# A selective scan with a third kind of state, one block for the activation functions of other tables, and Softplus and Silu taken from PSUM

## The chip, the cores and the metric

The kernel runs on one core of one Trainium2 chip. The metric is the device time of one execution in microseconds (us), taken over several runs. A core has a matrix engine (TensorE, PE in the profile), a vector engine (VectorE, DVE), an engine for activation functions (ScalarE, ACT), a general engine (GpSimd, POOL), and a queue that only issues transfers (SyncE, SP). Each engine works through its own instructions in the order in which the program put them there, and waits at an instruction until what it needs has been signalled by other engines. SBUF is the working memory, PSUM the small memory that TensorE writes into; it has eight banks of 128 x 512 f32.

## The reference

There are two layers with residuals. Layer 0 is a two-dimensional recurrent cell over a 64 x 64 image for 16 batches; the change does not touch it. Layer 1 is a bidirectional selective scan (Mamba) over the 4096 tokens of each batch, with 256 inner channels and 16 states per channel:

```python
xz = x @ in_w.T
xc, z = jnp.split(xz, 2, axis=-1)
# xc: causal convolution with 4 taps, + conv_b
xc = jax.nn.silu(...)
dbl = xc @ x_w.T
dt, Bm, Cm = jnp.split(dbl, [8, 24], axis=-1)
dt = jax.nn.softplus(dt @ dt_w.T + dt_b)
A = -jnp.exp(A_log)
dA = jnp.exp(dt[..., None] * A)
dBx = dt[..., None] * Bm[:, :, None, :] * xc[..., None]
# over the tokens:
h = dA_t * h + dBx_t
y = jnp.einsum('bds,bs->bd', h, C_t)
# then
y = (ys + xc * D) * jax.nn.silu(z)
return y @ out_w.T
```

The same is done on the reversed tokens, and both results are added. All is f32.

## The kernel before

Layer 1 cuts the tokens of a batch into 8 chunks of 512. One *pass* is one chunk in one direction: 16 batches x 2 directions x 8 chunks make 256 passes, the first 8 of a batch forward, the other 8 ("second") backward. A pass keeps the channels as 2 halves of 128 partitions, and treats the 16 states one after another. For state s it needs the decay exp(dt A) (two ScalarE instructions of 128 x 512, `decay`, line 482), the drive dt B x, two scans along the tokens on VectorE (`scan`, line 515), the product with C (`out_of`, line 539), and a sum over the states that TensorE makes by transposing each product into one PSUM accumulator `py` (`sums`, line 561, 8 transposes of 128 x 128).

Before, there are two kinds of state. Ten are *plain*: GpSimd multiplies dt x by the row of B (`drive`, line 492), the decay lies in PSUM (tag `da`, three banks), the scan writes `hst` into SBUF (two buffers), GpSimd multiplies by C, and ScalarE copies the last column into `carry` for the next chunk (`keep`, line 533). Six are *turned* (2, 4, 7, 9, 12, 15): ScalarE multiplies the transposed dt x by B as a scalar per partition (`drive_turned`, line 497, four instructions), TensorE turns the result back into two PSUM banks `hps` (`drive_back`, line 505, 8 transposes; there is one such tile), VectorE scans in place there with a decay in SBUF (`das`, two buffers), multiplies by C and copies the last column.

Around the states a pass does its own preparation one pass ahead: the convolution as 4 shifted matmuls for each half (`conv`), Silu on it in SBUF, `xproj` for dt, B and C, a round trip of B and C through DRAM, from where each row is spread over 128 partitions by a transfer on SP (`spread`, line 435), `dtproj`, Softplus in SBUF after an Identity that added the bias (lines 453 to 459), and dt x (`times`, on GpSimd). Second passes also make the gate z (copied from PSUM, then Silu in SBUF), add both directions and multiply by z (`finish`, two VectorE instructions; the forward passes copy `py` to `yf` on ScalarE instead), and project back.

Nothing is scheduled by a compiler: every step has a place, counted in states, in the tables `AT` and `STATE` (lines 639 to 682). All steps of all passes are put into one list, sorted by place, and issued in that order; so a table entry decides where an instruction stands in its engine's queue. The eight PSUM banks are `misc` 1, `da` 3, `hps` 2 and `py` 2.

Of the kernel before, what the change touches and what calls it, by code (L numbers as in the profile page):

```python
# [231 lines left out]
def layer1(tc, a, const, ident, group_norm, x1, out):  # L232
# [8 lines left out]
    with ExitStack() as ctx:  # L241
# [62 lines left out]

        TURNED = (2, 4, 7, 9, 12, 15)
        B_ROWS, C_ROWS = 6, 5
        PLAIN = tuple(s for s in range(NS) if s not in TURNED)

        def misc(name):
            return psum.tile([P, T], F32, name=name, tag="misc")
# [37 lines left out]
        class Pass:  # L350
            def __init__(self, b, n):
                self.b, self.n = b, n
                self.d, self.c = order[n]
                self.second = n >= NCH
                self.first = n % NCH == 0
                self.nm = f"{b}_{n}"
                self.rev = slice(None, None, -1 if self.d else 1)
                self.last = 0 if self.d else T - 1
                self.brow, self.crow, self.da, self.dbx, self.dbt = {}, {}, {}, {}, {}
                self.h, self.hlast, self.hc, self.das = {}, {}, {}, {}  # L360
                self.banks = set()
                self.added = 0
                self.py = None

# [13 lines left out]
            def conv_take(self, h):  # L378
                if h == 0:
                    self.xc = cp.tile([P, NH, T], F32, name=f"xc_{self.nm}", tag="xc")  # L380
                nc.scalar.activation(self.xc[:, h, :], self.pp, AF.Identity, bias=conv_b[:, h, :])  # L381

            def gate(self, i):

                pp = self.pp = psum.tile([P, 2, DI], F32, name=f"pz_{self.nm}_{i}", tag="misc")
                for j in range(2):
                    t0 = PAD + self.c * T + (2 * i + j) * P
                    nc.tensor.matmul(  # L388
                        pp[:, j, :],
                        lhsT=xT[self.b % 2][:, t0 : t0 + P],  # L390
                        rhs=in_wT[:, DI:],
                        start=True,
                        stop=True,
                    )

            def gate_take(self, i):
                if i == 0:
                    self.z = cp.tile([P, NB, DI], F32, name=f"z_{self.nm}", tag="z")
                nc.scalar.copy(self.z[:, 2 * i : 2 * i + 2, :], self.pp)

            def silu(self):
                nc.scalar.activation(self.xc, self.xc, AF.Silu)
                if self.second:
                    nc.scalar.activation(self.z, self.z, AF.Silu)

            def xproj(self):
                pd = self.pp = psum.tile([NDBL, T], F32, name=f"pd_{self.nm}", tag="misc")
# [33 lines left out]
                nc.sync.dma_start(t, src)  # L441

            def dtproj(self, h):
                pv = self.pp = misc(f"pv_{self.nm}_{h}")
                nc.tensor.matmul(  # L445
                    pv,
                    lhsT=dt_wT[:, h * P : (h + 1) * P],
                    rhs=self.dbl[:RANK, :],
                    start=True,
                    stop=True,  # L450
                )

            def dtproj_take(self, h):
                if h == 0:
                    self.dt = cp.tile([P, NH, T], F32, name=f"dt_{self.nm}", tag="dt")
                nc.scalar.activation(self.dt[:, h, :], self.pp, AF.Identity, bias=dt_b[:, h, :])  # L456

            def softplus(self):
                nc.scalar.activation(self.dt, self.dt, AF.Softplus)

            def times(self):
                self.dtx = cp.tile([P, NH, T], F32, name=f"dtx_{self.nm}", tag="dtx")
# [17 lines left out]


            def decay(self, s, h):
                if s in TURNED:
                    if h == 0:
                        self.das[s] = sp.tile([P, NH, T], F32, name=f"das_{self.nm}_{s}", tag="das")
                    t = self.das[s][:, h, :]
                else:
                    t = psum.tile([P, T], F32, name=f"da_{self.nm}_{s}_{h}", tag="da", bufs=3)
                nc.scalar.activation(t, self.dt[:, h, :], AF.Exp, scale=amat[:, h, s : s + 1])  # L489
                self.da[s, h] = t  # L490
# [24 lines left out]
            def scan(self, s):  # L515
                dbx = self.dbx.pop(s)
                if s in TURNED:
                    t = dbx
                else:
                    t = sp.tile([P, NH, T], F32, name=f"hst_{self.nm}_{s}", tag="hst", bufs=2)  # L520
                for h in range(NH):
                    nc.vector.tensor_tensor_scan(  # L522
                        t[:, h, self.rev],
                        self.da.pop((s, h))[:, self.rev],
                        dbx[:, h, self.rev],
                        0.0 if self.first else carry[:, self.d, h, s : s + 1],
                        ALU.mult,
                        ALU.add,
                    )
                self.h[s] = t  # L530
                self.hlast[s] = t

            def keep(self, s):
                (nc.vector.tensor_copy if s in TURNED else nc.scalar.copy)(
                    carry[:, self.d, :, s : s + 1],
                    self.hlast.pop(s)[:, :, self.last : self.last + 1],
                )
# [97 lines left out]
        def put(place, f, *args):  # L635
# [1 line left out]


        AT = {
            "conv": (-15.8, -14.5),  # L640
            "conv_take": (-14.7, -13.4),
            "gate": (-13.3, -12.8),
            "gate_take": (-12.9, -12.5),
            "silu": -12.27,
            "xproj": -10.87,
            "xproj_take": -10.08,
            "bturn": -9.79,
            "bturn_take": -9.49,
            "dtproj": (-9.25, -8.75),
            "dtproj_take": (-8.98, -8.48),  # L650
            "softplus": -8.17,
            "times": -6.08,
            "turn": (-5.39, -4.79),
            "turn_take": (-5.25, -4.34),
            "skip": (4.22, 4.93, 7.62, 8.2),
            "finish": 18.96,
            "residual": 15.49,
            "back": (19.6, 20.45),
            "back_take": (20.1, 20.7),
            "project": 24.0,  # L660
            "project_take": 24.49,
            "store": 25.98,
            "store_take": 26.48,
            "read_load": 3.57,
            "read_turn": 12.07,
            "read_take": 12.57,
            "normal": -2.75,
            "normalise": -1.31,
        }

        STATE = {
            "decay_turned": (-1.78, -1.23),
            "decay_plain": (-1.52, -0.92),
            "drive_turned": -2.2,
            "drive_back": -1.07,
            "out_turned": 0.16,
            "out_plain": 1.06,
            "keep_turned": 0.1,
            "keep_plain": 1.55,
            "sums_turned": 2.13,  # L680
            "sums_plain": 3.22,
        }

        plain = [(i, p, s) for i, p in enumerate(passes) for s in PLAIN]
# [2 lines left out]
        def many(i, p, name, n, f):  # L687
            for k in range(n):
                put(NS * i + AT[name][k], f, k)

        for i, p in enumerate(passes):
            at = NS * i
            many(i, p, "conv", NH, p.conv)
            many(i, p, "conv_take", NH, p.conv_take)
            if p.second:
                many(i, p, "gate", NB // 2, p.gate)
                many(i, p, "gate_take", NB // 2, p.gate_take)
            many(i, p, "dtproj", NH, p.dtproj)
            many(i, p, "dtproj_take", NH, p.dtproj_take)
            many(i, p, "turn", NB // 2, p.turn)  # L700
            many(i, p, "turn_take", NB // 2, p.turn_take)
            many(i, p, "skip", NB, p.skip)
            for name in ("silu", "xproj", "xproj_take", "bturn", "bturn_take", "softplus", "times"):
                put(at + AT[name], getattr(p, name))
            put(at + AT["finish"], p.finish)
            if p.second:
                many(i, p, "back", NH, p.back)
                many(i, p, "back_take", NH, p.back_take)
# [12 lines left out]
                        put(at + AT["normal"], normal, p.b + 1)  # L721
                    put(at + AT["normalise"], normalise, p.b + 1, p.n - NCH)
            for s in range(NS):
                kind = "turned" if s in TURNED else "plain"
                for h in range(NH):
                    put(at + s + STATE["decay_" + kind][h], p.decay, s, h)
                put(at + s, p.scan, s)
                put(at + s + STATE["keep_" + kind], p.keep, s)
                put(at + s + STATE["out_" + kind], p.out_of, s)
                put(at + s + STATE["sums_" + kind], p.sums, s)  # L730
                if s in TURNED:
                    put(at + s + STATE["drive_turned"], p.drive_turned, s)
                    put(at + s + STATE["drive_back"], p.drive_back, s)

        drive_at = []
        for k, (i, p, s) in enumerate(plain):
            if k < 2:
                at = NS * i + s - 2.5  # L740
            else:
                i2, _, s2 = plain[k - 2]
                at = NS * i2 + s2 + STATE["out_plain"] + 0.01
            drive_at.append(at)
            put(at, p.drive, s)
            ready = NS * i + AT["xproj_take"] + 0.01
# [1 line left out]
            put(max(ready, free), p.spread, "b", s)  # L748
        out_at = []
        for k, (i, p, s) in enumerate(every):  # L750
            out_at.append(NS * i + s + STATE["out_turned" if s in TURNED else "out_plain"])
            ready = NS * i + AT["xproj_take"] + 0.02
            free = out_at[k - C_ROWS] + 0.01 if k >= C_ROWS else ready
            put(max(ready, free), p.spread, "c", s)
# [40 lines left out]
```

## Time and profile before

| what | us |
|---|---|
| median of 3 runs | 15579.79 |
| lowest, highest | 15575.36, 15591.93 |
| the profiled execution | 15566.78 |
| its span on the core | 15565.0 |
| the first scan of layer 1 starts | 1623.3 |
| the last scan of layer 1 starts | 15544.0 |

The 256 passes lie between the two last entries: 13920.7 us, or 54.4 us for a pass. Busy shares of the engines over the span are PE 82%, DVE 87%, ACT 79%, POOL 82%; in a stretch of 1000 us of layer 1 alone (5000 to 6000) they are 80%, 89%, 83% and 89%. The granted clock of TensorE is 0.899 on average over the span. The DMA engines are busy 42% of that stretch. A profile of this kind lists for each group of instructions its line, engine, operation, output and input, count, then the busy time and the mean duration, then the idle time of the engine before it and what ended that idle time.

### The profile page before, as it was taken

The numbers are of one execution on the slowest core, as the hardware profiler recorded it, in microseconds if no ns is written. First come the engines' busy times: TensorE is split into PE (matmuls) and PEld (weight loads), VectorE is DVE, ScalarE is ACT, GpSimd is POOL, SyncE is SP. The second block draws the span as 40 slices with busy tenths as digits, with TensorE's granted clock in tenths as the row PEclk, the third lists the DMA queues.
The fourth block names the chain that finished last, engine by engine and source line by source line (L and its number), as shares of the span: only waits on it lengthen the run. The fifth ranks groups of instructions, "written<-read, shape, count | busy, mean of one in ns | idle before, by whom it ended". The sixth has DMA issues, their size and how long they took to land. (4 is left out here: it accounts for less than half of the span.)

```text
span 15565.0 us, 215358 instructions
## 1 busy us (share of the span) xinstructions
PE 12706.6 (82%) x68876; PEld 9322.4 (60%) x68876; DVE 13558.3 (87%) x14526; ACT 12256.2 (79%) x23207; POOL 12705.8 (82%) x5636
## 2 busy tenths in 40 slices
PE   8999778788878778887878888887878878787887
PEld 8658555556555555555555655555565655555555
DVE  6777789889898989899898989888898989898898
ACT  3444788888888888888888888888888888888887
POOL 0111889889898989899898989889898989899898
PEclk8999888888898988898889989888988988888998
DMA  3211444444444444444444444444444444444443
GB/s 115 55 54 43 130 129 138 132 136 135 131 139 128 142 128 139 131 137 136 131 139 128 142 128 139 132 134 134 135 136 131 142 129 139 129 138 133 133 135 121
DMA packets 1335631, 1978.89 MB, mean 127 GB/s; under 512 B 136664, under 2 KB 465888, under 8 KB 1334496
## 3 DMA queue, kind: packets, MB, share of 16 engines
q1 hardware_dynamic: 1256560, 1929.88, 39.1%
q10 hardware_dynamic: 77936, 35.23, 0.9%
q8 instruction: 546, 8.95, 0.2%
q14 instruction: 589, 4.83, 0.1%
HBM read 1880.69 MB, written 83.89 MB: 126 GB/s over the span
## 5 line engine op out<-in xcount | busy, mean ns | idle before, releaser
L543 POOL TENSOR_TENSOR hc<-hst,cr 128x1024 f32<-128x1024 f32 x2560 | 6047.6, 2362 | 1424.1 <-DVE hst L522 562.4
L494 POOL TENSOR_TENSOR dbx<-dtx,br 128x1024 f32<-128x1024 f32 x2560 | 6054.1, 2365 | 0.1
L522 DVE TENSOR_TENSOR_SCAN hst<-da,carry,dbx 128x512 f32<-128x512 f32 x4480 | 5475.8, 1266 | 462.1 <-ACT da L489 238.2
L551 PE MATMUL py<-ident,hc 128*128 128x128 f32 x32768 | 4409.1, 288 | 45.9 <-DVE y L582 40.5
L551 PEld LDWEIGHTS py<-ident,hc 128*128 128x128 f32 x32768 | 4039.9, 151 | 224.6 <-issue 187.7
L489 ACT ACTIVATE da<-dt,A_log_sb 128x512 f32<-128x512 f32 x5120 | 3443.4, 684 | 848.9 <-DVE hst L522 834.1
L522 DVE TENSOR_TENSOR_SCAN hps<-das,carry,hps 128x512 f32<-128x512 f32 x2688 | 3441.3, 1280 | 564.3 <-issue 224.6
L510 PE MATMUL hps<-ident,dbt 128*128 128x128 f32 x12288 | 2223.4, 323 | 884.0 <-DVE hc L543 452.0
L510 PEld LDWEIGHTS hps<-ident,dbt 128*128 128x128 f32 x12288 | 1701.9, 164 | 1582.5 <-ACT dbt L500 714.2
L500 ACT ACTIVATE dbt<-dtxt,bt 128x256 f32<-128x256 f32 x6144 | 2618.3, 499 | 0.0
L489 ACT ACTIVATE das<-dt,A_log_sb 128x512 f32<-128x512 f32 x3072 | 2113.0, 711 | 0.2
L370 PE MATMUL pp<-xT,wk 128*128 128x512 f32 x4096 | 1873.3, 600 | 190.6 <-ACT xc L381 188.3
L543 DVE TENSOR_TENSOR hc<-hps,cr 128x1024 f32<-128x1024 f32 x1536 | 1881.0, 1225 | 144.6 <-PE py L551 111.0
L370 PEld LDWEIGHTS pp<-xT,wk 128*128 128x128 f32 x4096 | 739.2, 190 | 985.7 <-issue 740.7
L196 POOL TENSOR_TENSOR a_f<-a_f,c 128x8 f32<-128x8 f32 (+31 forms) x254 | 199.3, 785 | 1348.4 <-ACT a_f L188 1172.1
L551 PEld LDWEIGHTS py<-ddiag,xc 128*128 128x128 f32 x4096 | 676.2, 231 | 366.0 <-issue 366.0
L470 PE MATMUL ptx<-ident,dtx 128*128 128x128 f32 x2048 | 372.2, 311 | 634.2 <-POOL dtx L463 382.8
L445 PE MATMUL pv<-dbl,dt_wT 8*128 8x512 f32 x1024 | 695.3, 764 | 199.5 <-ACT dt L456 199.2
L522 DVE TENSOR_TENSOR_SCAN hst<-da,dbx 128x512 f32<-128x512 f32 x640 | 742.5, 1206 | 112.6 <-ACT da L489 78.4
L551 PE MATMUL py<-ddiag,xc 128*128 128x128 f32 x4096 | 794.1, 326 | 0.0
L479 ACT COPY dtxt<-ptx 128x512 f32<-128x512 f32 x512 | 299.1, 584 | 551.2 <-PE ptx L470 550.8
L470 PEld LDWEIGHTS ptx<-ident,dtx 128*128 128x128 f32 x2048 | 270.6, 161 | 700.6 <-POOL dtx L463 417.9
(110 smaller groups left out, 13755.2 us busy)
## 6 DMA issues: line engine op xcount, KB each, us to landing
cr<-rows SPq DMA_DIRECT2D x4096, 256.0 KB
br<-rows SPq DMA_DIRECT2D x2560, 256.0 KB
xs<-in_x_dram SPq DMA_DIRECT2D x64, 512.0 KB
xl<-x SPq DMA_DIRECT2D x128, 256.0 KB
xr<-x SPq DMA_DIRECT2D x128, 256.0 KB
out_dram<-xr SPq DMA_DIRECT2D x128, 256.0 KB
xl<-in_x_dram SPq DMA_DIRECT2D x392, 64.0 KB
x<-xl ACTq DMA_DIRECT2D x392, 64.0 KB
```

What stands on the lines that cost most here:

```text
L196: nc.gpsimd.tensor_mul(f0, f0, cp[:, up, :])
L370: nc.tensor.matmul(pp, lhsT=wk[:, k, h * P : (h + 1) * P], rhs=xT[self.b % 2][:, t0 : t0 + T], start=(k == 0), stop=(k == TAPS - 1),)
L445: nc.tensor.matmul(pv, lhsT=dt_wT[:, h * P : (h + 1) * P], rhs=self.dbl[:RANK, :], start=True, stop=True,)
L470: nc.tensor.transpose(pt[:, j, h * P : (h + 1) * P], self.dtx[:, h, (2 * i + j) * P : (2 * i + j + 1) * P], ident,)
L479: nc.scalar.copy(self.dtxt[:, 2 * i : 2 * i + 2, :], self.pp)
L489: nc.scalar.activation(t, self.dt[:, h, :], AF.Exp, scale=amat[:, h, s : s + 1])
L494: nc.gpsimd.tensor_mul(t, self.dtx, bc(self.brow.pop(s), 1, NH))
L500: nc.scalar.activation(t[:, j, :], self.dtxt[:, j, :], AF.Copy, scale=self.bt[:, j, s : s + 1])
L510: nc.tensor.transpose(t[:, h, j * P : (j + 1) * P], dbt[:, j, h * P : (h + 1) * P], ident)
L522: nc.vector.tensor_tensor_scan(t[:, h, self.rev], self.da.pop((s, h))[:, self.rev], dbx[:, h, self.rev], 0.0 if self.first else carry[:, s ...
L543: eng.tensor_mul(t, self.h.pop(s), bc(self.crow.pop(s), 1, NH))
L551: nc.tensor.matmul(self.py[:, j, h * P : (h + 1) * P], start=j // 2 not in self.banks, stop=self.added >= (NS + 1 - 1) * NB * NH, skip_gro ...
```

## The change

Four states become a third kind, *mixed*: B on ScalarE and TensorE as for turned states, the scan from PSUM into SBUF, C on GpSimd as for plain states. Four are turned, four mixed, eight plain. `keep` of plain and mixed states is no longer a ScalarE copy but a transfer on SP. Silu of xc, Softplus and Silu of z stand in one block (`session`) in each pass, for three different passes; Softplus and Silu of z read PSUM directly, and their inputs take `misc` and one of the three `da` banks. `hst` has three buffers. All places are new; `finish` follows the last `sums`, and nothing that writes `py` for the next pass is put before it.

```diff
-        TURNED = (2, 4, 7, 9, 12, 15)
+        TURNED = (2, 8, 10, 14,)
+        MIXED = (0, 5, 7, 11,)
+        PLAIN = tuple(s for s in range(NS) if s not in TURNED and s not in MIXED)
...
             def gate_take(self, i):
...
-                nc.scalar.copy(self.z[:, 2 * i : 2 * i + 2, :], self.pp)
-            def silu(self):
-                nc.scalar.activation(self.xc, self.xc, AF.Silu)
-                if self.second:
-                    nc.scalar.activation(self.z, self.z, AF.Silu)
+                nc.scalar.activation(self.z[:, 2 * i : 2 * i + 2, :], self.pz[i], AF.Silu)
...
-            def dtproj_take(self, h):
-                nc.scalar.activation(self.dt[:, h, :], self.pp, AF.Identity, bias=dt_b[:, h, :])
             def softplus(self):
-                nc.scalar.activation(self.dt, self.dt, AF.Softplus)
+                for h in range(NH):
+                    nc.scalar.activation(
+                        self.dt[:, h, :], self.pv[h], AF.Softplus, bias=dt_b[:, h, :]
+                    )
...
             def decay(self, s, h):
-                if s in TURNED:
+                if s not in PLAIN:
...
-                    t = sp.tile([P, NH, T], F32, name=f"hst_{self.nm}_{s}", tag="hst", bufs=2)
+                    t = sp.tile([P, NH, T], F32, name=f"hst_{self.nm}_{s}", tag="hst", bufs=3)
...
             def keep(self, s):
-                (nc.vector.tensor_copy if s in TURNED else nc.scalar.copy)(
+                (nc.vector.tensor_copy if s in TURNED else nc.sync.dma_start)(
...
+        def session(i):
+            at = [passes[k] if 0 <= k < len(passes) else None for k in (i, i + 1, i + 2)]
+            if at[0] and at[0].second:
+                at[0].gate_take(0)
+            if at[1]:
+                at[1].dtproj(0)
+            if at[0] and at[0].second:
+                at[0].gate_take(1)
+            if at[2]:
+                at[2].silu()
+            if at[1]:
+                at[1].softplus()
...
-            many(i, p, "skip", NB, p.skip)
+            for j in range(NB):
+                put(max(at + AT["skip"][j], finished), p.skip, j)
...
+                summed = max(at + s + STATE["sums_" + k], finished)
+                lasts = max(lasts, summed)
+                put(summed, p.sums, s)
...
+            finished = lasts + 0.01
+            put(finished, p.finish)
```

The new tables, as far as the prediction speaks of them (places in states, from the pass's own first scan):

```diff
-            "conv": (-15.8, -14.5),
+            "conv": (-27.32, -26.22),
-            "finish": 18.96,
+            "session": 9.8,
...
-            "drive_back": -1.07,
-            "sums_turned": 2.13,
-            "sums_plain": 3.22,
+            "drive_mixed": -2.2,
+            "drive_back": -0.55,
+            "sums_turned": 1.95,
+            "sums_mixed": 3.94,
+            "sums_plain": 3.72,
```

## The prediction

> **What bounds the kernel now.** I read the page's busy shares first, then the busy time by windows, then the groups by line, then the timeline of two passes. The shares show no single bound.
>
> ```profile
> 5000.00:6000.00 1000.00, 801.47 (x4456) 588.61 (x4454) 894.35 (x855) 830.89 (x1553) 893.49 (x385) 0.90 0.42 135
> ```
>
> ```profile
> L543 POOL TENSOR_TENSOR hc<-hst,cr 128x1024 f32<-128x1024 f32 x2560 | 6047.6, 2362 | 1424.1 <-DVE hst L522 562.4
> L494 POOL TENSOR_TENSOR dbx<-dtx,br 128x1024 f32<-128x1024 f32 x2560 | 6054.1, 2365 | 0.1
> ```
>
> The window's columns are the busy us of PE, PEld, DVE, ACT and POOL, then clock, DMA share and GB/s. Of a pass of 54.4 us, DVE is busy 48.6 (89.4%), POOL 48.6, ACT 45.2, PE 43.6. POOL and DVE are equal, and each idles nearly 6 us, because they feed each other through two or three buffers and both hang on ACT. The timeline shows where a stall starts:
>
> ```profile
> 9019.05 1.28 ACT L402 ACT_TABLE_LOAD   x1
> ...
> 9020.35 1.06 ACT L402 ACTIVATE xc<-xc 128x1024 f32<-128x1024 f32 x1
> ...
> 9021.31 1.04 ACT L404 ACTIVATE z<-z 128x1024 f32<-128x1024 f32 x1
> ...
> 9022.37 1.28 ACT L489 ACT_TABLE_LOAD   x1
> 9023.66 1.30 ACT L489 ACTIVATE da<-dt,A_log_sb 128x512 f32<-128x512 f32 x2
> 9024.39 2.34 DVE L522 TENSOR_TENSOR_SCAN hst<-da,dbx 128x512 f32<-128x512 f32 x2 [1.98 <-ACT da L489]
> ...
> 9025.74 2.36 POOL L543 TENSOR_TENSOR hc<-hst,cr 128x1024 f32<-128x1024 f32 x1 [2.36 <-issue]
> ```
>
> For 4.6 us ACT makes no exponential; the scan then waits 1.98 us for its decay, and POOL 2.36 us for the scan. The same happens again at Softplus, so twice in a pass. The two halves of a batch differ, which the starts of the yf copies show:
>
> ```profile
> L578 ACT COPY yf<-py x8: 999/1001/1002, 8651.7 to 9015.7; 128x1024 f32<-128x1024 f32 x8
> ...
> L578 ACT COPY yf<-py x6: 999/1000/1002, 9522.3 to 9777.6; 128x1024 f32<-128x1024 f32 x6
> ```
>
> Seven intervals in the first line give 52.0 us for a forward pass. From 9015.7 to 9522.3 lie nine passes, mostly second ones: 56.3 us.
>
> **What the Trainium skill says.** "ScalarE: Activation LUTs", section "What ACT_TABLE_LOAD costs", has 1283 ns for a load, plus a drain of about 1380. The trace agrees on the load (1283) but shows no such drain: from load to next function is 1.30 us above. "GPSIMD Engine Reference", section "Performance versus the Vector engine", makes a two-input product 1.96 times as slow as on VectorE; here 2362 to 1225 ns, 1.93. "DMA: Bandwidth & Descriptors", section "Anatomy of one DMA", says a transfer has about 2.0 us of fixed cost and that the issuing sequencer, not the DMA engine, waits for semaphores. No transfer of 4-byte elements is in this trace; the rows of B and C take SP 0.32 us each to issue.
>
> **The change part by part**, in us per pass.
>
> *GpSimd.* 10 B + 10 C + dt x before, 8 B + 12 C + dt x after: 21 products either way. Back to back they start every 2.32 us (9028.06, 9030.39, 9032.70), so 48.7 is its floor before and after. Nothing is saved here.
>
> *VectorE.* Two turned states less: two products with C of 1.225 and two copies of 0.16, -2.8: 48.6 becomes 45.8. A mixed scan (decay SBUF, drive PSUM, result SBUF) isn't in the trace; its neighbours are 1.266 and 1.280, and I take 1.27, range zero to 0.03 each.
>
> *ScalarE.*
>
> ```profile
> L500 ACT ACTIVATE dbt<-dtxt,bt 128x256 f32<-128x256 f32 x6144 | 2618.3, 499 | 0.0
> ...
> L534 ACT COPY carry<-hst 128x2 f32<-128x2 f32 x2560 | 468.0, 183 | 1.9 <-DVE hst L522 1.9
> ...
> L489 ACT ACT_TABLE_LOAD x526 | 674.9, 1283 | 9.4
> ...
> L456 ACT ACTIVATE dt<-pv,dt_b_sb 128x512 f32<-128x512 f32 x512 | 351.9, 687 | 172.9 <-PE pv L445 172.7
> ...
> L459 ACT ACTIVATE dt<-dt 128x1024 f32<-128x1024 f32 x256 | 270.7, 1058 | 2.8
> ```
>
> B for two more states: 2 x 2618.3/1536 = +3.4. Ten copies of 0.183 leave: -1.8. Table loads fall from 1038 to 784 in layer 1 (counted in the built programs), 254 x 1.283/256 = -1.3. Softplus from PSUM costs the two Identities' 0.687 each and saves the 1.058: -1.1. Silu of z, in half the passes, saves 1.04: -0.5. Sum -1.3: 45.2 becomes 43.9. More important, the block is one. At place 9.8 it lasts 3 x 1.28 + 1.06 + 2 x 0.69 = 6.3, with z 7.5. Ahead of it ACT has made the decays of states 10 and 11 into the two `das` buffers and those of 9 into `da`; VectorE covers it with state 9 (2.4), 10 (3.9) and 11 (2.5), 8.8 us. So I cost the block at nothing; uncovered it would be about as much as each block costs now, 2 us.
>
> *TensorE.* Two more states of 8 transposes, 1.04 each when nothing is waited for: +2.1, 43.6 becomes 45.7.
>
> *SP.* Twelve `keep` transfers come in, two rows of B go. The wait for the scan now stands on SP, and rows of B and C queue behind it; those are ordered 9 us or more before their product, so a wait of a few us is covered. A scan that reuses a `hst` buffer waits for the `keep` of three users ago: the tightest are states 6 and 7, whose buffers were scanned about 5 us earlier. I take 2.0 us from the skill plus 1 us, an estimate, for 256 elements; hidden. The lower bound is no cost, the upper 1 us a pass if landing takes 6.
>
> *New waits.* There is one `hps` tile, and now 7-8 and 10-11 are neighbours that both use it. The second's transposes can start only when the first is scanned (or multiplied), with VectorE standing: 1.04 + 0.25 for the signals, 1.3, twice: +2.6. The profile of before has such a case ("1.26 <-PE hps"). VectorE then needs 48.4 on average, about 47.2 in a forward and 49.6 in a second pass (`finish` 2.45 and the residual 0.66 against 0.70 for the statistics).
>
> *The stretch from state 2 to state 7.* This is what I expect to set the end. `py` is single, so after the last `sums` TensorE has to wait for `finish`, which in second passes stands on VectorE between the scan of 2 and its product. In the built order it then does: skip and the first transpose of y (2.2), sums of 0 and 2 (1.75), transpose (0.44), hps of 5 (0.88), convolution (3.44), sums of 1 (0.88), convolution (3.44), hps of 7 (0.88). Durations are starts to starts at full clock: 0.88 for 8 transposes, 3.44 for a convolution.
>
> ```profile
> 9003.98 3.60 PE L370 MATMUL pp<-xT,wk 128*128 128x512 f32 x8
> ...
> 9020.44 1.04 PE L551 MATMUL py<-ident,hc 128*128 128x128 f32 x8
> ...
> 9207.87 1.91 PE L510 MATMUL hps<-ident,dbt 128*128 128x128 f32 x8
> ```
>
> That is 13.9 us, plus finish 2.5 and signals 0.5: scan 7 starts 16.9 after the scan of 2 ends. VectorE's own work in that time is 2.5 + 1.4 + 4 x 2.4 = 13.5, so it stands 3.4. The third line shows 8 transposes in 1.91 at half clock; at the window's mean of 0.90, 13.9 becomes 15.4 and scan 7 comes at 18.4. From scan 7 to the end of scan 2 of the next pass VectorE needs 37.1 (scans 2.4 plain, 2.5 mixed, 3.9 turned with its product, two stalls of 1.3, 0.6 for the residual). Second pass: 55.5. In a forward pass ACT empties `py`, the chain starts at the product of 2 and has 9.9 (11.0 at 0.90), with 1.0 of signals and ends; the rest of VectorE is 38.4: 50.4, over POOL's 48.7.
>
> The mean is 52.95, against 54.4: 1.45 x 256 = 370 less. From 15567 of the profiled execution that is 15197; the median of the runs is 13 above the profile, so about 15210.
>
> **The rivals.** *The stretch hides.* If the scans of 0 to 2 run ahead and TensorE loses nothing there, the floors count: POOL 48.7 and VectorE 49.6, with 1 us of friction for each: 50.2, 1075 less, 14500; half of it, 14850, is as likely. For it: ACT loses both stalls of 2 us shown above, POOL keeps its work and `hst` has a third buffer. Against it: transposes, convolution and skip stand in one queue in fixed order.
>
> *TensorE becomes the bound and the kernel is slower.* The mean pass is 39.75 + 11.9 k, k being how much longer TensorE takes in that stretch than at full clock. It passes 54.4 at k = 1.23, a clock of 0.81 there. At 0.75 a pass is 55.6, 15890. For it: transposes at half clock are seen above, and TensorE gets 2.1 us more. Against it: the mean over the window is 0.90.
>
> *Given back.* The gain at ScalarE is eaten by the `hst` wait for `keep` (up to 1 us) and the two hps stalls at half clock (2 x 0.9 in a fifth of the passes): 52.95 + 1 + 0.4, within 0.2% of before: 15560.
>
> **How the numbers follow.** The forecast gets 0.46, with an own range of 15000 to 15400; the stretch hides (whole or half) 0.28; slower 0.20; given back 0.06. A change under 0.2% can't be told from none here. That makes faster 0.74, same 0.06, slower 0.20. For 8 in 10 I cut half of the slower case and a third of the fast one: 14650 to 15700.
>
> **What would show it.** Right: the after profile has 784 loads, POOL's busy time unchanged, DVE's 700 us lower, scans of hps and mixed hst waiting for PE transposes, mostly in second passes, and few waits for da; forward passes near 50.4 and second ones near 55.5 by the yf copies. Wrong: DVE waiting for transfers at L539 (keep is late), or da waits at the block (it isn't covered), or POOL idle under 2 us a pass (the stretch hides).

## The result and the profile after

The changed kernel takes 15677.85 us (median of 4 runs, 15657.9 to 15701.39), the kernel before 15579.19 (15575.36 to 15591.93) beside it: a ratio of 1.0062, with a 95% interval of 1.0045 to 1.008. It is slower by 0.6%, where 2.4% faster was forecast. The profiled execution took 15681.59.

Every engine did about what the sums said. First the page's groups of GpSimd's two products, then the same 1000 us window as before (busy us of PE, PEld, DVE, ACT, POOL, then clock, DMA share, GB/s), both of the changed kernel:

```profile
L560 POOL TENSOR_TENSOR hc<-hst,cr 128x1024 f32<-128x1024 f32 x3072 | 7250.5, 2367 | 1510.4 <-PE py L568 714.7
L511 POOL TENSOR_TENSOR dbx<-dtx,br 128x1024 f32<-128x1024 f32 x2048 | 4855.2, 2371 | 0.1
```

```profile
5000.00:6000.00 1000.00, 814.72 (x4754) 618.17 (x4752) 832.59 (x774) 816.89 (x1477) 895.93 (x385) 0.91 0.44 125
```

VectorE lost 62 us of work in this window and now idles 167 of 1000 instead of 106; GpSimd is as busy as before. Nobody uses the time that came free. So some wait has taken its place, and the clock's mean (0.91 against 0.90) gives no hint where.

The starts of the `yf` copies say in which passes. These are the forward passes of two successive batches, from the view of one line's instructions:

```profile
L595 ACT COPY yf<-py x8: 1012/1012/1012, 4335.1 to 4714.8; 128x1024 f32<-128x1024 f32 x8
```

```profile
L595 ACT COPY yf<-py x8: 1012/1012/1012, 5219.2 to 5585.5; 128x1024 f32<-128x1024 f32 x8
```

Seven intervals each: 54.2 us for a forward pass in the first, 52.3 in the second. Over the 16 batches:

| us per pass | before | forecast | after |
|---|---|---|---|
| forward (mean of 16 batches) | 52.02 | 50.4 | 53.36 |
| second (mean of 15 intervals of nine passes) | 56.28 | 55.5 | 55.96 |

The second passes came out half a us above the forecast and below before. The forward passes failed.

A mean of seven intervals hides one thing. In the seventh VectorE also draws the statistics of the next batch together, 6.2 us from the first of these lines to the end of the second (the first of the two batches above):

```profile
4698.54 0.35 DVE L347 BATCH_NORM_AGGREGATE mv<-st 128x2 f32<-128x48 f32 x1
...
4704.58 0.16 DVE L83 SCALAR_TENSOR_TENSOR shift_l<-mean_l,scale_l 128x1 f32<-128x1 f32 x1
```

The first six intervals take 50.9 us in the kernel before and 52.5 in the changed one, the seventh 59.4 in both (means of 15 batches). The forecast of 50.4 is a sum without this step, so 50.9 was its proper neighbour, and not the 52.0 of the prediction.

One pass of the same batch shows what the forward passes wait for. This is TensorE's timeline from the transposes of state 8 to those of state 11 (start, us, engine, line, operation, and in brackets the idle time ahead and what ended it). The transposes of a state are those that turn its drive back into `hps` (L527); L568 are sums, L462 dt projections for the next pass, L334 transposes of the next batch's tokens:

```profile
4511.57 1.07 PE L527 MATMUL hps<-ident,dbt 128*128 128x128 f32 x8 [1.81 <-ACT dbt L517]
4512.48 2.04 PE L568 MATMUL py<-ident,hc 128*128 128x128 f32 x16
4516.89 1.90 PE L527 MATMUL hps<-ident,dbt 128*128 128x128 f32 x8 [2.37 <-ACT das L506]
4518.72 2.07 PE L462 MATMUL pv<-dbl,dt_wT 8*128 8x512 f32 x2
4520.73 1.97 PE L568 MATMUL py<-ident,hc 128*128 128x128 f32 x8
4522.62 2.07 PE L462 MATMUL pv<-dbl,dt_wT 8*128 8x512 f32 x2
4524.62 1.97 PE L568 MATMUL py<-ident,hc 128*128 128x128 f32 x8
4526.39 1.06 PE L334 MATMUL pt<-ident,xl 128*128 128x128 f32 x4
4527.24 1.91 PE L527 MATMUL hps<-ident,dbt 128*128 128x128 f32 x8
```

And VectorE's in the same place:

```profile
4516.59 0.15 DVE L551 COPY carry<-hps 128x2 f32<-128x2 f32 x1
...
4522.86 0.15 DVE L551 COPY carry<-hps 128x2 f32<-128x2 f32 x1
4529.25 2.45 DVE L539 TENSOR_TENSOR_SCAN hst<-das,carry,hps 128x512 f32<-128x512 f32 x2 [6.24 <-issue]
```

`hps` is free when VectorE has copied the last column of the state before: at 4516.7 from state 8, at 4523.0 from state 10. The transposes of 10 start at once; for them TensorE has waited 2.37 us (the profile names a decay, but the start fits the copy). Those of 11 start only at 4527.24, 4.2 us late, since dt projections, sums and the transposes of the next batch's tokens stand ahead of them and everything takes about twice its time: 8 transposes 1.9 us instead of 1.04. Scan 11 waits 6.24 us; "issue" only means that the profile saw no single event end the wait. In batches like the second above such a wait comes in every other pass (5.2 us in one, 1.3 in the next). Over all 128 forward passes scan 11 waits 4.6 us on average.

Half speed comes in whole pieces of 3.41 us. Here is the stretch cut at those borders, in the same columns as the window above:

```profile
4510.11:4513.53 3.42, 1.96 (x17) 1.83 (x18) 2.11 (x3) 3.42 (x8) 3.42 (x3) 1.00 0.45 142
4513.53:4516.94 3.41, 1.04 (x9) 0.83 (x10) 3.27 (x5) 3.02 (x7) 3.41 (x2) 1.00 0.36 104
4516.94:4520.35 3.41, 3.41 (x10) 1.95 (x10) 3.35 (x3) 3.36 (x4) 3.38 (x2) 0.50 0.47 123
4520.35:4523.77 3.42, 3.42 (x11) 2.06 (x10) 2.58 (x3) 0.72 (x1) 0.94 (x1) 0.50 0.54 148
4523.77:4527.18 3.41, 3.41 (x14) 2.56 (x13) 0.00 (x0) 2.43 (x3) 3.41 (x2) 0.50 0.18 68
4527.18:4530.59 3.41, 3.41 (x18) 3.41 (x17) 1.34 (x2) 3.40 (x8) 2.64 (x2) 0.50 0.58 187
4530.59:4534.01 3.42, 3.34 (x30) 3.00 (x28) 3.42 (x4) 1.22 (x3) 2.18 (x1) 1.00 0.05 2
```

In the second window TensorE is busy 1.04 us. Then come four at half clock, although it is busy all the time in them. Counted over 600 such windows in each profile (2048 us of layer 1): after a full-speed window with under 1.5 us busy the next was at half clock in 48 of 51 cases (49 of 51 in the kernel before), after one with 1.5 us or more in 17 of 433 (43 of 423). So the clock falls after TensorE has been idle. And it comes back after a window whose weight loads (the second number) fill 3 us or more: always, 117 of 117 in both profiles; otherwise in 41 of 123.

The exceptions have something in common too: the dt projections, whose matmuls use 8 of 128 rows. Leave their time out of TensorE's busy time, and the windows of layer 1 fall apart cleanly (8126 in both profiles together):

| time without dt projections | next window at half speed |
|---|---|
| full-speed window, under 1.25 us | 658 of 658 |
| full-speed window, 1.75 us or more | 14 of 5013 |
| half-speed window, under 2.5 us | 495 of 495 |
| half-speed window, 3 us or more | 2 of 1103 |

The dt projections reach into the first three of the four half-speed windows above. So two things go with half speed here: idle time, which starts it in this pass, and dt projections, which prolong it. That the eight rows are the reason is not shown, since no run changes them. The convolution, as wide as the dt projections but on 128 rows, does count: of 1392 full-speed windows with 1 us or more of it 3 were followed by half speed.

"TensorE: Matmul & The Clock Gate" of the Trainium skill, section "What's actually happening", describes this: a free-running window of 3413 ns, half speed after an idle window, full speed after a busy one. The window's length agrees. Its "idle" and "busy" can't be read off the busy time as it stands: the window with 1.04 us of work was followed by half speed here, and so were three windows full of work, a part of it dt projections.

### The profile page after: what moved, and what is told of

Same layout as the page of the kernel before. It is cut to its first block, busy times and chain, and to the rows that moved or that the text cites. A ratio compares the mean times of both kernels' runs of the same rounds, so it can differ in the third digit from the quotient of the medians.

```text
span 15679.8 us, 226417 instructions
## 1 busy us (share of the span) xinstructions
PE 12915.4 (82%) x72972; PEld 9750.6 (62%) x72972; DVE 12767.0 (81%) x13502; ACT 12038.9 (77%) x22058; POOL 12722.8 (81%) x5636
## 5 line engine op out<-in xcount | busy, mean ns | idle before, releaser
L560 POOL TENSOR_TENSOR hc<-hst,cr 128x1024 f32<-128x1024 f32 x3072 | 7250.5, 2367 | 1510.4 <-PE py L568 714.7
L511 POOL TENSOR_TENSOR dbx<-dtx,br 128x1024 f32<-128x1024 f32 x2048 | 4855.2, 2371 | 0.1
L539 DVE TENSOR_TENSOR_SCAN hst<-da,carry,dbx 128x512 f32<-128x512 f32 x3584 | 4360.7, 1263 | 563.4 <-ACT da L506 382.1
L568 PEld LDWEIGHTS py<-ident,hc 128*128 128x128 f32 x32768 | 4147.1, 155 | 738.4 <-issue 615.5
L568 PE MATMUL py<-ident,hc 128*128 128x128 f32 x32768 | 4573.1, 296 | 38.5 <-POOL hc L560 34.7
L506 ACT ACTIVATE da<-dt,A_log_sb 128x512 f32<-128x512 f32 x4096 | 2754.2, 680 | 958.9 <-DVE hst L539 955.5
L517 ACT ACTIVATE dbt<-dtxt,bt 128x256 f32<-128x256 f32 x8192 | 3474.6, 497 | 2.0 <-PE hps L527 1.8
L527 PE MATMUL hps<-ident,dbt 128*128 128x128 f32 x16384 | 2378.1, 293 | 1284.3 <-DVE carry L551 664.3
L527 PEld LDWEIGHTS hps<-ident,dbt 128*128 128x128 f32 x16384 | 1994.7, 151 | 1903.9 <-ACT da L506 625.6
L539 DVE TENSOR_TENSOR_SCAN hst<-das,carry,hps 128x512 f32<-128x512 f32 x1792 | 2187.7, 1262 | 1003.9 <-issue 459.1
L506 ACT ACTIVATE das<-dt,A_log_sb 128x512 f32<-128x512 f32 x4096 | 2788.0, 712 | 49.6 <-DVE hps L539 49.5
L539 DVE TENSOR_TENSOR_SCAN hps<-das,carry,hps 128x512 f32<-128x512 f32 x1792 | 2294.0, 1280 | 388.8 <-ACT da L506 163.9
L568 PE MATMUL py<-ddiag,xc 128*128 128x128 f32 x4096 | 739.9, 346 | 738.3 <-DVE y L599 597.3
L560 DVE TENSOR_TENSOR hc<-hps,cr 128x1024 f32<-128x1024 f32 x1024 | 1252.4, 1223 | 30.3
L568 PEld LDWEIGHTS py<-ddiag,xc 128*128 128x128 f32 x4096 | 671.3, 252 | 794.6 <-issue 623.5
L462 PE MATMUL pv<-dbl,dt_wT 8*128 8x512 f32 x1024 | 753.5, 823 | 3.7
L480 POOL TENSOR_TENSOR dtx<-dt,xc 128x1024 f32<-128x1024 f32 x256 | 607.1, 2372 | 73.9 <-ACT dt L474 73.9
```

What stands on the lines that cost most here:

```text
L462: nc.tensor.matmul(pv, lhsT=dt_wT[:, h * P : (h + 1) * P], rhs=self.dbl[:RANK, :], start=True, stop=True,)
L480: nc.gpsimd.tensor_mul(self.dtx, self.dt, self.xc)
L511: nc.gpsimd.tensor_mul(t, self.dtx, bc(self.brow.pop(s), 1, NH))
L517: nc.scalar.activation(t[:, j, :], self.dtxt[:, j, :], AF.Copy, scale=self.bt[:, j, s : s + 1])
L527: nc.tensor.transpose(t[:, h, j * P : (j + 1) * P], dbt[:, j, h * P : (h + 1) * P], ident)
L539: nc.vector.tensor_tensor_scan(t[:, h, self.rev], self.da.pop((s, h))[:, self.rev], dbx[:, h, self.rev], 0.0 if self.first else carry[:, s ...
```

## The experiments

Three theories: QUEUE, the order of TensorE's work around states 10 and 11 makes scan 11 late; COLD, the half clock after idle time does; KEEP, the carry transfers on SP hold `hst` and the rows.

**TensorE's order around state 11.**

```diff
+        LATE = {6: -0.3, 8: 0.52}
-            "read_turn": 10.19,
+            "read_turn": 10.5,
-                summed = max(at + s + STATE["sums_" + k], finished)
+                summed = max(at + s + STATE["sums_" + k] + LATE.get(s, 0), finished)
```

> Against the changed kernel (15678) only TensorE's order around states 10 and 11 differs: the sums of 6 stand before the transposes of 10, the sums of 8 and the transposes of the next batch's tokens behind those of 11. Theory QUEUE (scan 11 waits because at half clock about 10 us of sums, dt projections and token transposes stand between the transposes of 10 and 11): the wait of scan 11 in forward passes falls from 6.3 or 1.3/5.3 in turn to 2.5 or less, forward passes take about 50 us, second passes 0 to 1 less; total 15680 - 3.3 x 128 = 15250, 15100 to 15400. Theory KEEP (the carry transfers on SP hold hst buffers and the rows): same passes as the changed kernel, 15640 to 15720.

Measured: 15561.71, ratio to the kernel before 0.9989 (0.998 to 0.9997). Forward passes 52.20, second 55.99. Scan 11 waits 2.18 us on average in forward passes, so the queue was part of it and 0.7% came back, a quarter of what was expected. The clock did not come back: 130 of 600 windows at half speed, 124 in the changed kernel. But it falls for another reason now. The two dt projections stand together, and the window that holds them is followed by half speed although TensorE is busy 2.55 us in it:

```profile
4388.32 1.98 PE L462 MATMUL pv<-dbl,dt_wT 8*128 8x512 f32 x4
```

```profile
4387.75:4391.16 3.41, 2.55 (x10) 1.07 (x8) 3.31 (x4) 3.36 (x4) 3.41 (x3) 1.00 0.37 124
4391.16:4394.57 3.41, 0.98 (x5) 1.01 (x6) 2.25 (x3) 3.37 (x5) 3.41 (x2) 0.50 0.58 163
```

Of the falls to half speed in forward passes, 107 of 130 come after a window that was busy 1.5 us or more, with at least 0.5 us of dt projections; in the changed kernel 24 of 152. So the run changed the order and the cause of the half clock at once, and doesn't part the two.

**The carry copies back on ScalarE.**

```diff
-                (nc.vector.tensor_copy if s in TURNED else nc.sync.dma_start)(
+                (nc.vector.tensor_copy if s in TURNED else nc.scalar.copy)(
```

> The changed kernel with the carry copies of plain and mixed states on ScalarE again. KEEP: scans lose waits of 'issue', forward passes come to 51, second ones to 55.5; total about 15400. QUEUE: ScalarE gets 12 x 0.18 = 2.2 us a pass more and its decays come later; forward passes no better than 52.3, total 15650 to 15900.

Measured: 16883.36, 1.0841 (1.0822 to 1.0859), worse than any theory said. The list of waits shows that it isn't the copies' 593.6 us of work:

```profile
ACT carry L551 <- DVE hst L539: 3081.3, 2424, 4.3
```

The columns are the total us, the times and the longest. A copy placed half a state behind its scan stands at the head of ScalarE's queue until the scan ends, with all decays behind it. In the kernel before it stood 1.55 states behind, and waited 1.9 us in all. On SP the same wait harms nobody: the transfers of the changed kernel wait 2603.0 us there for scans, and none of its scans is listed as waiting for a transfer. KEEP is out, and with these places the copies can't stay on ScalarE; other places for them weren't tried.

**More work for TensorE, where it idles.**

```diff
+            def filler(self):
+                pf = misc(f"pf_{self.nm}")
+                for j in range(16):
+                    nc.tensor.transpose(pf[:, :P], ident, ident)
...
             if p.second:
                 many(i, p, "gate", NB // 2, p.gate)
+            else:
+                put(at + 9.43, p.filler)
```

> The changed kernel with 16 transposes of the identity (1.75 us at full clock), whose result nobody reads, put before the transposes of 10 in forward passes, where TensorE idles 2.3 us. Theory COLD (TensorE's clock halves for a window of 3.41 us after a window in which it was busy less than about 1.5 us, and this lands on the queue before scan 11): more work makes the kernel faster; fewer half-clock windows at scans 10 and 11, forward passes 51 to 52, total 15680 - 1.8 x 128 = 15450, 15350 to 15600. QUEUE without COLD (the clock falls for another reason, such as load): the queue is 1.75 longer, forward passes 1 to 2 us slower, 15800 to 15950. KEEP: same or up to 0.5% slower.

Measured: 15293.83, 0.9819 (0.9805 to 0.9834). Transposes that nobody reads make the kernel 2.4% faster than the changed one, and 1.8% faster than the one before. Forward passes take 50.54 us. That this is so near the forecast's 50.4 is luck: the first six intervals of a batch take 49.5 us, the seventh 57.3. TensorE's timeline in the same place of a forward pass, then the scan of 11:

```profile
3618.59 1.91 PE L396 MATMUL pf<-ident 128*128 128x128 f32 x16
3621.12 1.06 PE L532 MATMUL hps<-ident,dbt 128*128 128x128 f32 x8 [0.63 <-ACT das L511]
3622.12 1.12 PE L467 MATMUL pv<-dbl,dt_wT 8*128 8x512 f32 x2
3623.17 1.09 PE L573 MATMUL py<-ident,hc 128*128 128x128 f32 x8
3624.19 1.12 PE L467 MATMUL pv<-dbl,dt_wT 8*128 8x512 f32 x2
3625.24 1.09 PE L573 MATMUL py<-ident,hc 128*128 128x128 f32 x8
3626.17 0.60 PE L334 MATMUL pt<-ident,xl 128*128 128x128 f32 x4
3627.39 1.07 PE L532 MATMUL hps<-ident,dbt 128*128 128x128 f32 x8 [0.62 <-DVE carry L556]
```

```profile
3628.55 2.45 DVE L544 TENSOR_TENSOR_SCAN hst<-das,carry,hps 128x512 f32<-128x512 f32 x2 [1.31 <-issue]
```

The order is that of the changed kernel, with the filler ahead. The queue that took 10.35 us from the transposes of 10 to those of 11 takes 6.3, TensorE now waits for `hps` instead of the other way round, and scan 11 waits 1.31. Over all forward passes its mean wait falls from 4.6 us to 1.5, and a forward pass gets 2.8 us shorter, so this wait is about all that the filler removed. Windows at half clock: 81 of 600.

**The same filler elsewhere**, behind the transposes of 11 (place 10.46 instead of 9.43).

> The changed kernel with the same 16 transposes a forward pass, put behind the transposes of 11 instead of before those of 10. COLD with its place: the window ahead of the transposes of 10 stays nearly idle, the queue up to the transposes of 11 runs at half clock as before, and the work comes on top: 15650 to 15900. If any more work on TensorE keeps the clock up, wherever it stands: 15300 to 15450.

Measured: 16051.01, 1.0302 (1.0287 to 1.0318). Forward passes take 56.42. The place makes the difference; the size was a little more than expected, because the filler now delays the transposes of dt x as well (scan 14 waits 2.9 us on average, where the timeline names `dtxt`), and scan 11 still waits 4.7.

**A quarter of it**: 4 transposes instead of 16.

> The changed kernel with 4 filling transposes (0.44 us) a forward pass instead of 16, at the same place. COLD with a threshold near 1.5 us busy in a window of 3.41 (the windows ahead show 1.58): part of the windows gets over it, between 15294 and 15678, about 15450. If 16 work only because they fill the idle time fully: 15640 to 15720.

Measured: 15584.48, 1.0004 (0.9996 to 1.0013). Between the changed kernel and 16 transposes, as COLD says, but nearer the former than expected: forward passes 53.02, and scan 11 waits 3.9 us on average. That fits windows at the edge of 1.5 us that are pushed over it only at some times.

**The same remedy for the kernel before**: 16 transposes where it idles 3.2 us, waiting for dt x.

```diff
+            if not p.second:
+                put(at + 10.6, p.filler)
```

> The kernel before with 16 transposes of the identity in forward passes before the first turn of dt x, where TensorE idles 3.2 us and a half-clock window follows. If the clock after idle time is what limits both kernels alike: 1 to 2% faster, 15280 to 15430. If it limits only the changed kernel, because there the cold windows fall on a queue that VectorE waits for, while in the kernel before VectorE and GpSimd are the limit in forward passes: within 0.5%, 15500 to 15650. I expect the latter.

Measured: 15604.89, 1.0016 (1.0009 to 1.0023). The kernel before has as many cold windows (123 of 600) and gains nothing in this place. But the filler hardly raised the clock there: 0.902 on average against 0.900, and over layer 1 820 of 4080 windows at half speed against 841 of 4068. So the run doesn't tell what half speed costs the kernel before. For slack speaks its own trace: in the second to seventh pass of a batch its scans wait 2.9 us a pass in all, those of the changed kernel 8.0. That the change took slack away is likely by that, and not shown.

**The transfers in the kernel before.** Its ten ScalarE copies become transfers on SP, with two `hst` buffers.

> The kernel before with nothing changed but the carry copies of its ten plain states, which become transfers on SP (hst keeps two buffers). KEEP: scans wait for hst, whose buffers come free some 2 us later; with two buffers more than with three: 1 to 5% slower, 15750 to 16350. QUEUE/COLD: ScalarE has 1.8 us a pass less, the transfers are hidden by GpSimd's product, which holds hst longer anyway: within 1%, 15450 to 15650.

Measured: 17780.06, 1.1414 (1.1397 to 1.1431). The list of waits:

```profile
DVE hst L522 <- DMA carry<-hst: 2521.7, 937, 5.7
```

A scan that waits for the buffer does so for 2.7 us on average. In the changed kernel no scan is listed as waiting for such a transfer. It has a third buffer, but it also orders the transfer half a state behind its scan instead of 1.55, and SP works in order:

```profile
SPq L441 <- POOL hc L543: 5371.2, 2237, 6.3
```

So rows that wait for GpSimd stand ahead of the transfers here. Which of the two hides them in the changed kernel, the buffer or the place, wasn't tried.

**A filler for the second passes too**: 28 transposes in front of `skip`, where TensorE waits 4.4 to 5.4 us for `finish`.

```diff
+            if i and passes[i - 1].second:
+                put(finished, passes[i - 1].filler, "s", 28)
             for j in range(NB):
                 put(max(at + AT["skip"][j], finished), p.skip, j)
```

> The run with 16 transposes of the identity before the transposes of 10 in forward passes, and also 28 of them (3.1 us at full clock) in front of skip after each second pass, where TensorE idles 4.4 to 5.4 us while finish runs on VectorE. COLD: the half-clock window that now follows finish (a window of 3.4 us at the start of skip, sums and the transposes of 5) is gone, scan 5 waits 1 us less or not at all; second passes 54 to 55 us instead of 55.4, total 15294 - 128 x 1 = 15150, 15000 to 15250. Without COLD: same or slower, 15290 to 15400.

Measured: 15059.04, 0.9664 (0.9649 to 0.9678). Second passes 53.82, forward 50.56; 46 of 600 windows at half clock.

**What sets the second passes.** The last runs worked on the way from `finish` to the transposes of 7 and 8. The first, on the forward filler alone, moves the second half of the convolution behind the transposes of 7 in all passes:

```diff
-            "conv": (-27.32, -26.22),
-            "conv_take": (-26.5, -25.0),
+            "conv": (-27.32, -25.53),
+            "conv_take": (-26.5, -24.8),
```

> The run with the filler before the transposes of 10 in forward passes, with the second half of the convolution moved behind the transposes of 7 and its copy on ScalarE from place 6.0 to 7.2. Theory STRETCH (in second passes the second decay of 6 stands behind that copy, which waits for the convolution: scan 6 waits 3.4 us, scan 7 0.6): these waits go, scan 8 waits up to 1 us more; second passes 53, forward ones as they are or 1 less; total 15294 - 128 x 2.4 = 14990, 14850 to 15150. If what comes next in the queue takes its place (transposes of 8, the gate): 15200 to 15350.

Measured: 15370.43, 0.9865 (0.9849 to 0.9882), slower than without: second passes fell to 54.54, forward ones rose to 52.31. (The copy's old place was 7.0, and not 6.0.) The wait of 3.44 us for the decay of 6 stayed, since it stands behind the copy of the *first* half; I had taken the wrong one. In forward passes scan 8 waited up to 3.5 instead.

The next moves that decay ahead of the copy, with both fillers:

```diff
-                    put(at + s + STATE["decay_" + k][h], p.decay, s, h)
+                    put(at + s + STATE["decay_" + k][h] - (0.47 if (s, h) == (6, 1) else 0), p.decay, s, h)
```

> The run with both groups of filling transposes, and the second decay of state 6 put before the copy of the convolution and before B of 8 on ScalarE (0.47 of a state earlier). Theory COPY (scan 6 stands 3.0 us for this decay, which is queued behind that copy, which waits 1 us for TensorE): the wait falls to under 0.5 us, second passes 51.5 to 52.5 instead of 53.9, since scan 7 then waits longer for its transposes; total 15059 - 128 x 1.9 = 14815, 14700 to 14950. If TensorE's queue up to the transposes of 7 sets the pace alone: 15000 to 15080.

Measured: 15066.82, 0.9674 (0.966 to 0.9688): no gain. The wait at the decay of 6 is gone and appears at scan 7:

```profile
4904.91 2.45 DVE L544 TENSOR_TENSOR_SCAN hst<-das,carry,hps 128x512 f32<-128x512 f32 x2 [4.17 <-POOL hc L565]
```

The line names a product of GpSimd, but TensorE's transposes of 7 run from 4903.79 to 4904.82 in that pass, behind the convolution, and the scan starts 0.09 us later. One more on that base puts the sums of 8 and the token transposes behind the transposes of 11.

> The run before this one, with the sums of 8 and the transposes of the next batch's tokens behind the transposes of 11 as in the first experiment. QUEUE: scan 11's waits of 1.3 to 2.1 us are those of one hps tile at full clock (1.3), so at most 0.8 a pass is to be had in passes that are still cold there: 0 to 150 less. If GpSimd, busy 94% of the time with both fillers, is the limit by now: no change.

Measured: 15269.47, 0.9802 (0.9786 to 0.9819), 1.3% slower: with the order that had helped alone, forward passes take 52.01 us instead of 50.56, with 7.1 us of half clock each instead of 3.5. As in the first experiment the dt projections stand together: 75 of 130 falls to half speed in forward passes come after a window that was busy 1.5 us or more with dt projections in it, 24 of 83 without that order. A filler is tied to the order around it.

With the convolution's second half behind the transposes of 7 in passes that begin with `finish` only, and then also the sums of 3 and the projection behind the transposes of 8:

```diff
-            many(i, p, "conv", NH, p.conv)
-            many(i, p, "conv_take", NH, p.conv_take)
+            late = i >= 3 and passes[i - 3].second
+            for k in range(NH):
+                put(at + (-25.53 if late and k else AT["conv"][k]), p.conv, k)
+                put(at + (-24.8 if late and k else AT["conv_take"][k]), p.conv_take, k)
```

> The run with both fillers and the earlier decay of 6, and in passes that begin with finish the second half of the convolution behind the transposes of 7 (its copy from place 7.0 to 7.2). STRETCH (TensorE's queue from finish to the transposes of 7 sets the second pass, as the wait of 3.7 to 4.2 us of scan 7 in the last run says): that wait falls by the convolution's 3.4 us, scan 8 gets up to 1 us more; second passes 51 to 52 instead of 53.9, forward ones unchanged at 50.7; total 15067 - 128 x 2.4 = 14760, 14650 to 14900. If the wait only moves on to the transposes of 8 and 10: 15000 to 15100.

```diff
-            "project": 23.43,
+            "project": 23.47,
-                summed = max(at + s + STATE["sums_" + k], finished)
+                summed = max(at + s + STATE["sums_" + k] + (0.74 if s == 3 and i and passes[i - 1].second else 0), finished)
```

> The last run, with the sums of 3 and the projection of the pass before behind the transposes of 8 in passes that begin with finish. STRETCH: scan 8's wait of 4.6 us falls by the 2.7 us of these two; second passes 51.5 to 52.5 instead of 53.8, total 15062 - 128 x 1.8 = 14830, 14700 to 14950. If it again only moves (to GpSimd, whose products are 48.7 of a second pass and which waits 3.2 us for sums on TensorE, or to the sums of 3 for the product of 8): 14980 to 15080.

Measured: 15061.65, 0.9669 (0.9653 to 0.9685), then 14968.43, 0.9611 (0.9595 to 0.9627). VectorE's wait in a second pass, first of the one, then of the other:

```profile
4903.37 2.68 DVE L544 TENSOR_TENSOR_SCAN hps<-das,carry,hps 128x512 f32<-128x512 f32 x2 [4.61 <-PE hps L532]
```

```profile
4880.06 2.68 DVE L544 TENSOR_TENSOR_SCAN hps<-das,carry,hps 128x512 f32<-128x512 f32 x2 [1.85 <-PE hps L532]
...
4894.48 2.45 DVE L544 TENSOR_TENSOR_SCAN hst<-das,carry,hps 128x512 f32<-128x512 f32 x2 [3.47 <-POOL dbx L516]
```

The first line of each is scan 8, the last one scan 11. VectorE's wait went from the decay of 6 to the transposes of 7 and then of 8 as the items were moved, and only the last step brought a gain: 4.61 became 1.85. More than half of that went to scans 10 and 11, so second passes fell from 53.84 to 53.22, not to 52. TensorE's queue is one thing that second passes wait for; how much of the rest is GpSimd's, busy 946 of 1000 us in this run, was not separated. This is the fastest version seen, 3.9% faster than the kernel before and 4.5% faster than the changed one (14968.43/15677.85).

## Why the prediction was wrong

*Work per engine: right.* GpSimd 12705.8 and 12722.8 us (the 1.96 that the prediction takes from "GPSIMD Engine Reference" is stated there for an addition; the products here came to 1.93). VectorE -791 (forecast 2.8 x 256 = 717), a mixed scan 1.262 us (1.27 taken). ScalarE -217 (333), with 785 table loads at the four lines of layer 1.

*The block at nothing: right in effect.* GpSimd's dt x waits for Softplus 73.9 us in all. In slow passes Softplus itself waits 3.7 us for its dt projection on the half-speed TensorE, still under cover.

*Transfers hidden: right*, with the third buffer and the earlier place. The 2.0 us that the prediction takes from "DMA: Bandwidth & Descriptors" of the Trainium skill, section "Anatomy of one DMA", is stated there for transfers that GpSimd issues. These are issued by SP, and no run here shows how long one takes. Their worth was mis-sized: I credited 1.8 us a pass of ScalarE work, but with these places the copies on ScalarE would cost 8%.

*The stretch from 2 to 7 in second passes: right in size*, 55.96 for 55.5, and in that TensorE's queue sets it. The last link was another. In the changed kernel scan 7 waits 0.6 us only; scan 5 waits 1.8 for its transposes, and the second half of scan 6 waits 3.4 for a decay that ScalarE makes behind the convolution's copy. The "few waits for da" did not come true there. Moving the items took the wait on to the transposes of 7, and then of 8.

*"New waits: 1.3, twice": this step failed.* It priced scan 11's wait as one group of transposes plus signals, at full clock, with TensorE standing ready. For scan 8 it is that: 1.31 on average. For scan 11 it was forecast at 1.3 and measured at 4.6 in forward passes (1.9 in second ones), and at 1.5 with the filler. For between the transposes of 10 and 11 the table put two dt projections, two sums and the token transposes. The 2.4 us idle ahead of them, in which TensorE waits for `hps` from state 8, starts half speed for all of it, the dt projections go with its lasting, and the wait is 6.3 us, or 1.3 and 5.3 in turn. I put the clock into the sum as a mean of 0.90 over the other stretch. The mean was right (0.90 before and after) and useless: half speed is not spread out, it follows idle time and dt projections, and so it falls on the queue behind a wait.

The sum of the misses: forward 53.36 - 50.4 = 2.96, times 128 is 379; second 0.46 x 128 = 59; layer 1's first scan starts 17 us later (1640.8). Together 455 of the 485 between 15197 and the profiled 15681.59. Of the 2.96 us, scan 11 is 3.2 in the first six intervals, and the longer seventh interval, for which the forward sum has no term, adds about 1.0. The rest of a pass came out 1.1 below the forecast.

*The rival "TensorE becomes the bound"* had the sign and the half clock, but the wrong reason. It put the half clock into the stretch behind `finish` and had more work on TensorE speak for it; the half clock that cost the time fell between the transposes of 10 and 11, and more work in the right place made the mean clock rise to 0.934 and 0.955.

## What to carry over

Look for TensorE's clock in short windows, not as a mean, and ask what stands in its queue just after each idle time: that is what will run at half speed, and if another engine waits for it, the idle time is paid twice. Ask also which work counts: by the counts above, time spent on the dt projections was as good as idle. Before pricing a new wait, list all that the queue holds between the buffer's release and the instruction that reuses it. An operation that must wait belongs on a queue where nobody in a hurry stands behind it: the same 128 x 2 copies were nearly free on SP in the changed kernel, cost 8% on ScalarE at the same places, and 14% on SP in the kernel before, with two buffers and a later place.

## What the hardware showed

The clock is 1.00 or 0.50 over whole windows of 3.413 us, free-running against the program. Under 1.5 us of work in a full-speed window brought half speed in the next in 97 of 102 cases. A window full of work doesn't always bring full speed back: half-speed windows busy for 3.3 us or more were followed by full speed in 946 of 946 cases without dt projections in them, and in 22 of 299 with 0.5 us or more of them. Of full-speed windows with 1 us or more of dt projections all 216 were followed by half speed in the kernel before, and 110 of 221 in the changed one. Section "HAM oscillation — how this bites in real kernels" of the same page of the skill puts the limit at gaps of over 3.4 us; here a gap of 2.4 us inside one window was enough.

Passes seem to lock to these windows. In the run that moved the sums of 8 with both fillers, the later forward passes of a batch start 51.3 us apart and their half-clock episodes 51.2, which is 15 windows, and the changed kernel settles into 52.3 or 54.2 us for the forward half of most batches. What picks between the two was not tried.
